# Causal attentions of a decoder: the order of weights, row maxima, roots, values and context turns

## The chip, the cores and the metric

The kernel runs on one core of a Trainium2 chip. The metric is the device time of one execution in microseconds (us). The kernel before was run three times; a further execution was profiled. TensorE multiplies matrices (PE in the profile, PEld for its weight loads), VectorE (DVE), ScalarE (ACT) and GpSimd (POOL) do elementwise work and reductions, and SyncE's queue (SP) issues most DMAs.

## The reference

Eight sequences of 256 tokens with 512 features pass through two decoder layers with post-norm: x = layernorm(x + f(x)) six times. Three of the six functions are causal attentions, and the change is in these:

```python
# 0: differential attention, 16 heads of two 16-wide queries each, 4 key heads
scores = jnp.einsum('bhqd,bhkd->bhqk', q, k) * scale
scores = jnp.where(causal, scores, jnp.finfo(scores.dtype).min)
probs = jax.nn.softmax(scores, axis=-1)
attn_out = jnp.einsum('bhqk,bhkd->bhqd', probs, v)
attn = attn_out[:, 0::2] - lambda_full * attn_out[:, 1::2]
attn = attn * jax.lax.rsqrt(jnp.mean(attn * attn, axis=-1, keepdims=True) + EPS) * ln_w
...
# 3: self attention, 16 heads of 32
a = jax.nn.softmax(scores, axis=-1)
ctx = jnp.einsum('bhqk,bhkd->bhqd', a, v)
...
# 5: attention with keys and values chosen per token by a gate (top 1 of 16)
att = jnp.einsum('bhqd,bkd->bhqk', q, k_shared) * (1.0 / math.sqrt(hd))
y = jnp.einsum('bhqk,bkd->bhqd', jax.nn.softmax(masked, axis=-1), v_shared)
```

Between them stand a long convolution with gating by a context (1), a mixture of eight experts (2) and an attention over context and tokens (4). Everything is in float32.

## The kernel before, in words

The 2048 tokens are 16 tiles of 128. A group (g) is four tiles, so two sequences; there are four groups. All three causal attentions go through one function, `causal_attention` (L1094), each with its own `prepare` (projections of a group) and `finish` (output projection of a sequence, residual, norm). The attentions are called "first" (differential), "second" (self) and "third" (routed) below.

The unit of work is four heads of one sequence. The first attention has 8 units a sequence (`upb`), the others 4; so there are 64, 32 and 32 units. The order of work inside is written out by hand (`manual_schedule`): a loop over slots u, one slot for each unit and some more at the end, says what each engine gets next. Each engine takes its instructions in the order in which the loop issues them.

A unit passes through three steps in different slots:

- `maxima(u)` (L1140): 12 small products give the scores of 4 heads in the PSUM tile ps_q (L1148). ScalarE copies them to `rows` (L1157), GpSimd masks the diagonal blocks (L1159), and VectorE takes negated row maxima (`largest`, L1168) into `neg`. `rows` has two buffers in the first attention and one in the other two.
- After the last unit of a sequence, `split` (L1172) has VectorE write the maxima as three bfloat16 terms, and `turn` (L1185) has TensorE turn them (ps_n, L1190) and ScalarE copy them to `negT` (L1198).
- `weights(u)` (L1200): TensorE makes the transposed scores and adds the turned maxima (ps_k, L1211 and L1220), ScalarE takes the exponential to `pT` (L1228), and GpSimd masks it (L1229) and adds two blocks (L1239). ps_q and ps_k share one PSUM buffer of four banks.
- `products(u)` (L1241): TensorE multiplies with the values (L1254) and with ones for the sums (L1264), into ps_pv, which has one buffer; VectorE takes the reciprocal (L1272) and multiplies (L1278, or L367 and L370 in the first attention).

In slot u the kernel before issues maxima of unit u, then a first part of filling work, the turn (if a sequence has just ended), `sums(u)` (the products of unit u - upb - 1), the row maximum of unit u, the split, what is registered for "mid", the weights of unit u - upb, and the rest of the filling work, then what is registered for "end".

Filling work is TensorE work between the steps. It comes as lists of steps: projections of the next group (`feature_block` and `token_block`, four products of 128x512 each, L182), turns of token tiles (L194, copied by ScalarE, L195), and output projections (ps_o). `fill(budget)` issues steps until a budget per slot is spent, which spreads a group's work over its slots; `need(slot)` issues at once all that is due. Filling projections share three PSUM buffers (the pool `pools`, tag "mm") with turned tiles and ps_n. `begin(g)` asks `prepare` for a group's pieces, half a group ahead.

In the first attention `values` (L323) is due in slot 9 of its group; `turn_context` (L355) in the last group turns the 16 tiles of the context and stores them for a later stage, due in slots 0 to 15. Each tile is loaded by SP into one of two buffers (cx), turned, copied and stored by SP.

`norm_later` (L148) takes moments on VectorE and then the root on GpSimd (`rsqrt`, L140 and L141), and returns the last operation (L154) for later. `add_norm_later` (L208) adds the residual (L211) first. So the two GpSimd operations stand in GpSimd's queue wherever the output projection ended. In the second attention the tokens themselves arrive from the expert stage: `combine` (L1065) gives `load`, `add` (L1081) and a norm.

## Time and profile before

| | us |
|---|---|
| median of 3 runs | 2251.23 |
| lowest and highest | 2244.91 and 2252.63 |
| the profiled execution | 2256.86 |
| its span, first to last instruction | 2255.2 |
| its mean granted TensorE clock | 0.957 of full speed |
| first attention, about | 0 to 500 |
| second attention, about | 1175 to 1545 |
| third attention, about | 1885 to 2255 |

A line of a group in the profile names the source line, the engine, the operation, and the tiles written and read; then follow the number of instructions, their busy time and mean duration, and the idle time of the engine just before them with what ended it. A line of waits has the waiting instruction, what released it, the total in us, the number of waits and the longest. A line of the timeline has start and duration in us, and in brackets the engine's idle time before it. A product in float32 is counted as two instructions there. "PE busy" is modelled for the end of each product.

The groups that are particular to the attentions:

| group | instructions | mean us |
|---|---|---|
| L1157, copy of scores (ACT) | 128 | 1.44 |
| L1228, exponential (ACT) | 128 | 1.45 |
| L1159, mask of rows (POOL) | 128 | 1.10 |
| L1229, mask of pT (POOL) | 128 | 1.09 |
| L1239, sum of two blocks (POOL) | 112 | 1.28 |
| L1168, row maximum (DVE) | 128 | 1.75 |
| L1272, reciprocal (DVE) | 128 | 1.75 |
| L140, first operation of the root (POOL) | 80 | 0.22 |

### The profile page before, as it was taken

To read this page: it belongs to the slowest core of one execution; us is meant where nothing else is said; L and a number is where in the kernel's file an instruction comes from. 1 tells how busy PE (TensorE), PEld (TensorE's weight loads), DVE (VectorE), ACT (ScalarE), POOL (GpSimd) and SP (SyncE) were. 2 spreads that over 40 slices of the span, in tenths; PEclk is the share of its full clock that TensorE was granted. 3 is DMA by queue.
4 is the path that set the end of the run, shared out by engine and by line. 5 is a ranking of instruction groups with operands and counts; after the bars stand their busy time and mean duration, and the time that the engine had idled before them with its cause. 6 is when DMAs were issued, how large, how long until landed. Compare 5 with 4: busy or idle time off the path is not lost. (4 is left out here: it accounts for less than half of the span.)

```text
span 2255.2 us, 35573 instructions
## 1 busy us (share of the span) xinstructions
PE 2072.2 (92%) x14904; PEld 1204.6 (53%) x14904; DVE 1272.1 (56%) x1923; ACT 600.0 (27%) x723; POOL 820.2 (36%) x918
## 2 busy tenths in 40 slices
PE   7889888788999999999959999998999999999996
PEld 4454555444444456555524444446877875545553
DVE  4677666557888964122224656456343343566787
ACT  4555455420000013111114333330110111333332
POOL 2576666555555823000024445333000000232343
PEclk8999999798999999999979999989999999998898
DMA  6899702205214135131131102002000100000000
GB/s 226 339 383 381 260 27 84 73 1 169 83 59 147 57 112 178 61 137 64 47 133 36 58 28 66 1 1 94 29 28 19 38 1 1 1 10 10 10 20 29
DMA packets 110032, 197.56 MB, mean 88 GB/s; under 512 B 7088, under 2 KB 30768, under 8 KB 109872
## 3 DMA queue, kind: packets, MB, share of 16 engines
q1 hardware_dynamic: 104752, 178.49, 23.0%
q0 software_dynamic: 5120, 16.78, 2.2%
q8 instruction: 120, 1.97, 0.4%
q14 instruction: 40, 0.33, 0.0%
HBM read 93.54 MB, written 112.20 MB: 91 GB/s over the span
## 5 line engine op out<-in xcount | busy, mean ns | idle before, releaser
L1272 DVE RECIPROCAL rsum<-ps_pv 128x256 f32<-128x256 f32 x128 | 224.4, 1753 | 290.5 <-PE ps_pv L1264 290.4
L171 PE MATMUL ps_y<-kv,wt 128*128 128x512 f32 x640 | 282.4, 599 | 4.6 <-POOL kv L516 3.8
L1228 ACT ACTIVATE pT<-ps_k 128x1536 f32<-128x1536 f32 x128 | 185.6, 1450 | 303.1 <-PE ps_k L1220 303.1
L1168 DVE TENSOR_REDUCE neg<-rows 128x12 f32<-128x1536 f32 x128 | 223.5, 1746 | 64.9 <-POOL rows L1159 64.9
L1157 ACT COPY rows<-ps_q 128x1536 f32<-128x1536 f32 x128 | 184.1, 1438 | 182.8 <-PE ps_q L1148 153.6
L1229 POOL TENSOR_SCALAR_AFFINE_SELECT pT<-pT 128x1024 f32<-128x1024 f32 x128 | 139.6, 1091 | 240.1 <-ACT pT L1228 239.9
L1159 POOL TENSOR_SCALAR_AFFINE_SELECT rows<-rows 128x1024 f32<-128x1024 f32 x128 | 140.1, 1095 | 221.7 <-ACT rows L1157 221.0
L171 PEld LDWEIGHTS ps_y<-kv,wt 128*128 128x128 f32 x640 | 120.7, 192 | 154.7 <-issue 135.0
L1239 POOL TENSOR_TENSOR pT<-pT 128x512 f32<-128x512 f32 x112 | 143.0, 1277 | 9.3
L1074 POOL DMA_INDIRECT w_l1x<-ys,slots x32 | 31.5, 985 | 267.1 <-DMA ys<-y_m 259.2
L140 POOL TENSOR_SCALAR rstd<-bn_mv 128x1 f32<-128x1 f32 x80 | 17.3, 217 | 299.7 <-DVE bn_mv L146 293.0
L182 PE MATMUL ps_f<-xT,w_l1a 128*128 128x512 f32 x256 | 121.6, 619 | 3.9 <-ACT xT L195 3.9
L182 PE MATMUL ps_t<-w_l1f,xT 128*128 128x512 f32 x256 | 119.8, 606 | 0.1
L989 PE MATMUL po_m<-dn,hT 128*128 (+1 forms) x216 | 101.9, 609 | 1.6
L1264 PE MATMUL ps_pv<-pT,ones_v 128*32 128x256 f32 (+1 forms) x1152 | 88.9, 393 | 10.1 <-POOL pT L1239 9.9
L554 DVE TENSOR_REDUCE yc<-z 128x64 f32<-128x512 f32 x128 | 86.1, 674 | 6.2 <-POOL w_l1a L555 5.8
L182 PEld LDWEIGHTS ps_f<-xT,w_l1a 128*128 128x128 f32 x256 | 47.7, 195 | 58.6 <-issue 51.7
L182 PE MATMUL ps_o<-w_l,yT_b 128*128 128x512 f32 x128 | 69.8, 660 | 9.9 <-DVE yT_b L467 9.3
L1148 PEld LDWEIGHTS ps_q<-kz,qT 32*128 32x128 f32 x1536 | 50.8, 193 | 51.4 <-ACT pT L1228 35.7
L1148 PE MATMUL ps_q<-kz,qT 32*128 32x128 f32 x1536 | 63.3, 296 | 15.4 <-ACT pT L1228 11.8
L1211 PE MATMUL ps_k<-qT,kT 32*128 32x256 f32 (+1 forms) x1024 | 73.6, 374 | 3.9 <-ACT pT L1228 3.4
L1148 PEld LDWEIGHTS ps_q<-kT,qT 32*128 32x128 f32 x1536 | 49.8, 190 | 48.9 <-issue 28.7
(326 smaller groups left out, 3712.4 us busy)
## 6 DMA issues: line engine op xcount, KB each, us to landing
xs<-zero SPq DMA_DIRECT2D x8, 4352.0 KB, 31.4
ys<-zero SPq DMA_DIRECT2D x8, 4352.0 KB, 31.4
filters<-in_L_xattn_k SPq DMA_DIRECT2D x4, 2560.0 KB
first_h<-xs SPq DMA_DIRECT2D x36, 256.0 KB, 2.7
ys<-y_m SPq DMA_DIRECT2D x36, 256.0 KB, 2.0
gu<-in_L_ffn_gate_up_proj SPq DMA_DIRECT2D x3, 2816.0 KB, 20.1
wt<-filters SPq DMA_DIRECT2D x32, 256.0 KB, 2.9
x<-in_x SPq DMA_DIRECT2D x16, 256.0 KB, 4.4
```

The source lines that it names most:

```text
L171: nc.tensor.matmul(ps, lhsT=lhsT(k), rhs=rhs(k), start=(k == 0), stop=(k == n - 1))
L182: nc.tensor.matmul(ps[0], lhsT=lhsT(k), rhs=rhs(k), start=(k == 0), stop=(k == KB - 1))
L989: nc.tensor.matmul(po, lhsT=hT[:m, i, :], rhs=dn[i][:m, bass.ds(e, 1), :], start=(i == 0), stop=(i == len(FCH) - 1),)
L1148: nc.tensor.matmul(block[:, s, j, :], lhsT=q(rows, c, b * S + i * P, P), rhs=k(rows, c, b * S + keys * P, P), start=True, stop=True,)
L1157: nc.scalar.copy(d.rearrange("p j s k -> p s j k"), block)
L1159: nc.gpsimd.affine_select(out=rows, in_=rows, compare_op=ALU.is_ge, fill=-FAR, base=0, pattern=[[0, 8], [-1, P]], channel_multiplier=1,)
L1168: return lambda: nc.vector.tensor_reduce(neg[u // upb % 2][:, :, :, c], d, AX.X, ALU.max, negate=True)
L1228: nc.scalar.activation(p[:, 0:3].rearrange("p j s q -> p s j q"), block, AF.Exp)
L1229: nc.gpsimd.affine_select(out=p[:, 0:2].rearrange("p j s q -> p (j s) q"), in_=p[:, 0:2].rearrange("p j s q -> p (j s) q"), compare_op=ALU ...
L1239: nc.gpsimd.tensor_tensor(p[:, 3], p[:, 1], p[:, 2], ALU.add)
L1264: nc.tensor.matmul(ps[32 * s : 32 * s + 32, 1, j * P :], lhsT=ones_v, rhs=p[:, 1, s, :] if j else first[:, :, s, :], start=(j == 0), stop= ...
L1272: nc.vector.reciprocal(r, ps[:, 1, :])
```

## The change

- The weights of a unit come upb + 1 slots behind its maxima (before: upb), and its products a slot behind that (upb + 2). Each attention has one slot more at its end.
- Inside a slot the order becomes: maxima, first filling work, sums, "mid", weights, begin of a group, turn, rest of the filling work, row maximum, split, "end".
- In the slots after the last unit the weights come ahead of the turn and the sums.
- `norm_later` takes an argument that puts the root elsewhere: in the attentions it is registered for "end" of the slot.
- In the first attention, from the second group on, `values` is the first piece after the turned tiles, and v has three buffers; the 16 context turns are due six slots later.
- In the third attention one more query block is issued ahead of the turn of the keys.

```diff
-    def norm_later(dst, src):
+    def norm_later(dst, src, later=lambda f: f()):
...
-        rsqrt(rstd, mv[:, 1:2], 1.0)
+        later(lambda: rsqrt(rstd, mv[:, 1:2], 1.0))
...
-    def add_norm_later(work, t, ps):
+    def add_norm_later(work, t, ps, at):
...
-        return norm_later(x[t], r)
+        at(1, "mid", norm_later(x[t], r, lambda f: at(0, "end", f)))
...
-            v = work.tile([P, TPG, P], F32, tag="v", name="v")
+            v = work.tile([P, TPG, P], F32, tag="v", name="v", bufs=3)
...
+            values_steps = [(MM, lambda ti=ti: values(ti)) for ti in range(TPG)]
+            if g:
+
+                need.append((0, values_steps))
...
-            need.append((9, [(MM, lambda ti=ti: values(ti)) for ti in range(TPG)]))
+            if g == 0:
+                need.append((9, values_steps))
...
-                    need.append((t, [(TR, lambda t=t: turn_context(work, pools, t))]))
+                    need.append((6 + t, [(TR, lambda t=t: turn_context(work, pools, t))]))
...
-            lag = upb + 1
+            wait = upb + 1
+            lag = wait + 1
...
-                if u >= units:
-
+                if u < units:
+                    largest = maxima(u)
+                    short = min(0.3 * rate, 0.8)
+                    if rate > 2.7:
+                        short += (rate - 2.7) / 2
+                    left = fill(left + short)
+                    sums(u)
+                    happen("mid")
+                    if u >= wait:
+                        weights(u - wait)
+                    if u % upg == upb and u // upg + 1 < NG:
+                        per_group = begin(u // upg + 1)
+                    if u and u % upb == 0:
+                        turn(u // upb - 1)
+                    left = fill(left + rate - short - MM)
+
+                    need(u + 1)
+                    left = fill(left + MM)
+                    largest()
+                    if u % upb == upb - 1:
+                        split(u // upb)
+                else:
+
+                    if u < units + wait:
+                        weights(u - wait)
                     if u == units:
-                        sums(u)
                         turn(B - 1)
-                    if u < units + upb:
-                        weights(u - upb)
-                    if u > units:
-                        sums(u)
+                    sums(u)
                     happen("mid")
                     left = fill(left + rate)
-                    happen("end")
-                    continue
-                largest = maxima(u)
-                if u % upg == upb and u // upg + 1 < NG:
-                    per_group = begin(u // upg + 1)
-                short = min(0.3 * rate, 0.8)
-                if rate > 2.7:
-                    short += (rate - 2.7) / 2
-                left = fill(left + short)
-                if u and u % upb == 0:
-                    turn(u // upb - 1)
-                sums(u)
-                largest()
-                if u % upb == upb - 1:
-                    split(u // upb)
-                happen("mid")
-                if u >= upb:
-                    weights(u - upb)
-                left = fill(left + rate - short - MM)
-
-                need(u + 1)
-                left = fill(left + MM)
                 happen("end")
...
-                    at(first - here + 1, "mid", add)
+                    at(first - here + 1, "mid", lambda add=add: add(lambda f: at(0, "end", f)))
...
-            need.append((0, feature_block(pools, qT, xT, wqkv, 0, 1, HD1**-0.5)))
+            for c in range(1, 3):
+                need.append((0, feature_block(pools, qT, xT, wqkv, 0, c, HD1**-0.5)))
             need.append((0, [(TR, keys_turned)]))
-            for c in range(2, KB):
+            for c in range(3, KB):
                 need.append((c, feature_block(pools, qT, xT, wqkv, 0, c, HD1**-0.5)))
```

## The prediction

> **What bounds the kernel now.** I read the page first, for the engine that is busy throughout; then the table of windows by stage, which gives TensorE's idle time and clock in each; then the waits of TensorE stage by stage; then the timeline of single slots; and last the order of the instructions on each engine in the two kernels.
>
> ```profile
> span 2255.2 us, 35573 instructions
> PE 2072.2 (92%) x14904; PEld 1204.6 (53%) x14904; DVE 1272.1 (56%) x1923; ACT 600.0 (27%) x723; POOL 820.2 (36%) x918
> ```
> ```profile
> core 0: us, PE busy (x) PEld busy (x) DVE busy (x) ACT busy (x) POOL busy (x), PEclk, DMA share, GB/s
> 0.00:500.00 500.00, 425.33 (x5463) 250.17 (x5464) 314.76 (x353) 237.62 (x226) 297.25 (x299) 0.95 0.56 200
> ...
> 1175.00:1545.00 370.00, 346.81 (x2949) 168.93 (x2947) 204.33 (x264) 129.30 (x132) 150.42 (x170) 0.97 0.10 29
> ...
> 1885.00:2255.00 370.00, 333.92 (x3056) 182.82 (x3056) 243.48 (x342) 115.49 (x112) 118.25 (x126) 0.92 0.03 13
> ```
>
> The three causal attentions fill 0 to 500, 1175 to 1545 and 1885 to 2255 us. TensorE is idle in them for 75, 23 and 36 us, and it runs at 0.95, 0.97 and 0.92 of its clock. Only these 134 us, and what slow clock follows them, can be won: the change adds and removes no instruction (the counts of every kind on every engine are equal in the two orders). TensorE's waits in the first stage, one line of the second and two of the third:
>
> ```profile
> PE ps_n L1190 <- DVE terms L1179: 12.0, 6, 2.7
> PE ps_q L1148 <- ACT pT L1228: 11.8, 14, 1.6
> PE ps_o L182 <- DVE yT_b L467: 9.3, 4, 4.3
> ```
> ```profile
> PE ps_pv L1254 <- POOL pT L1229: 9.5, 6, 2.7
> ```
> ```profile
> PE pt_k L1681 <- DVE k L1676: 4.6, 2, 2.3
> PE pt L194 <- DVE sel L1665: 2.7, 1, 2.7
> ```
>
> One slot that turns a batch's maxima, from the timeline:
>
> ```profile
> 205.52 0.95 PE L1148 MATMUL ps_q<-kz,qT 32*128 32x128 f32 x24
> ...
> 206.63 1.18 DVE L1175 TENSOR_TENSOR neg<-neg 128x32 f32<-128x32 f32 x1
> ...
> 209.74 0.20 DVE L1179 CAST terms<-less 128x64 bf16<-128x64 f32 x1
> ...
> 209.99 0.40 PE L1190 MATMUL ps_n<-ident_b,terms 128*32 128x128 bf16 x8 [2.46 <-DVE terms L1179]
> ...
> 210.18 1.50 PE L1254 MATMUL ps_pv<-pT,v 128*32 128x256 f32 x16
> ...
> 213.89 1.45 ACT L1228 ACTIVATE pT<-ps_k 128x1536 f32<-128x1536 f32 x1 [3.07 <-PE ps_k L1220]
> ```
>
> (The cast shown is the last of three; the lines left out on VectorE are the others and the subtractions.) VectorE splits the maxima from 206.6 to 209.9; TensorE stands 2.46 us, then does the 16 products of L1254 in 1.50 us, where the slot before took 0.86 us at 200.70. This slot lasts 10.08 us, from 205.52 to the next L1148 at 215.60. Its neighbours last 6.3 to 7.0.
>
> An ordinary slot is a ring through the one score buffer: 12 maxima products 0.95, copy L1157 1.44, 16 weights products about 1.25, exp L1228 1.45, and small gaps. The shortest slots, such as 228.91 to 234.36, last 5.45 us. From the order I added up each slot as 0.9 + the larger of 1.65 and the products between maxima and weights + 1.25 + the larger of 1.65 and the products behind the weights, with 0.88 us for a filling step of 128x512 and 1.5 us for a slot's L1254 and L1264. All slots but the last of each attention (and the very first) give 366, 312 and 271 us for the kernel before. The timeline has 414 (25.71 to 440.07), 326 (1177.71 to 1503.90) and 297 (1916.01 to 2212.95). So 48, 14 and 26 us are stalls and slow clock.
>
> **What the Trainium skill says.** "TensorE: Matmul & The Clock Gate", Part 1, says that idle time costs twice: after a window of about 3.4 us with little work TensorE falls to half its clock. The 1.50 us against 0.86 us after the stall agrees. "PSUM — Partial Sum Buffer", Engine vs sequencer instructions, says that the queues of ScalarE, VectorE and GpSimd are strictly first in, first out, so an instruction that waits holds up all behind it. The root at 1283.07 below, ahead of a mask whose input was ready, agrees. "SBUF — State Buffer", Who interferes with whom, says that VectorE and GpSimd lock one shared pair of ports. It fits a split operation that takes 1.18 us beside GpSimd's work (206.63) where a like one takes 0.22 us alone, and is why I leave the split's 3.3 us as they are.
>
> **The change part by part.**
>
> *Turn behind the weights.* In the first attention six turns waited for "terms", about 2.5 us in four of the ordinary ones (slots 16, 24, 32, 56: 2.69, 1.54, 2.46, 2.46 = 9.2 us). Behind each, L1254, L1264 and L1211 took 1.50, 1.07 and 0.91 us where 0.86, 0.61 and 0.71 are usual: 1.3 us, times four is 5.2. Gross 14.4 us. In the changed order the turn follows products and weights, some 4 us into the slot, beside the exp. The split then starts behind the maximum at a slot's end: reciprocal from 2.9 us into the slot, 1.76 + 0.45 + 1.75 + 3.3 ends 10.2 us after the slot began, 3.9 us into the next. So it fits barely. I take 4 us back for late turns (bounds 0 and 9). The turn at slot 8 has no products ahead of it in either order and keeps its 2.7 us. Net 10.
>
> *Maximum at the slot's end.* VectorE's adds (L211), which free the filling products' buffers, and the scaling by the roots (L467) now come before the 1.75 us maximum and the split of their slot. The stalls on them were 3.2 us (ps_f at slot 47) and 4.3 us (slot 40). I take 7 of these in the first attention, 2 of 3.0 in the second (bounds 0 and all).
>
> *Values first.* Their first product needs only the first turned tile, where the keys' product waited 1.6 us for the last copy, twice (slots 25 and 42). Gain 3 (0 to 3.2). The third buffer of 2 KB costs no time.
>
> *Context in the last slots.* Stalls for cx were 5.2 us of waits. The new order has three runs of three or four turns in slots 53, 58 and 59 through the same two buffers; two in a row are covered and a third waits for its load. Loads and stores go through SP's queue as before. I take a gain of 1 (bounds -3 and +5).
>
> *One slot further behind.* The sum over slots is unchanged in the first attention (366 and 366): one full slot becomes a maxima-only one, and unevenness eats the rest (one slot has 7.0 us behind its weights, two have none). But one round of weights, exp, mask and products moves into the tail, where nothing fills it. Rounds there last 3.5 to 5.3 us (456.57, 460.51, 463.97, 469.24): 4.5 us lost, and 1.5 us for the turn at the stage's end, which again meets the split. First attention: 10 + 7 + 3 + 1 - 6 = 15 us gained.
>
> *Roots at the end.* GpSimd waited for bn_mv 293 us in all. At 1283.07 it does so ahead of the mask of pT whose exp had ended long before, and the products stand behind it. They lost 9.5 and 2.7 us to pT in the second attention; I take 5. The root's wait at a slot's end holds only the next slot's mask of rows, which needs a copy 2.5 us into that slot. The second attention gains 2 more at its first turn (1.6 us of wait in the slot from 1208.63). Its slot sum falls from 312 to 307, but 4.1 us of that are ps_o steps that go to the tail: gain 1. The extra round costs 3.5. Rows have one buffer here, so a copy waits for the maximum of the slot before; a slot has 5.1 us before its weights, 3.5 before the copy must start, so I take 1. Second attention: 5 + 2 + 2 + 1 - 3.5 - 1 = about 6 gained.
>
> *Third attention.* pt_k waited 2.3 us twice and the clock fell; another query block (4 x 0.88 us) now lies ahead of it: gain 5. The slots that turn tokens and compute gates (from 1940.92, 2024.57, 2113.65) take 15.3, 21.4 and 16.7 us against 9.6, 11.1 and 8.5 by the sum; the turns come behind the weights now, where exp and not the split holds their buffers. I take 7 of 24 (bounds -5 and 15). Costs: the query block ahead of the first maxima 3.5, less 0.7 from the slot sum; two slots with nothing to fill them (the fourth of a group) where the weights would be ready 2.6 us in but the copy waits for the late maximum, 2.5 each, 5; the extra round at the kernel's very end 4, its turn 1. Net 12 - 12.8, about 1 lost.
>
> Sum: 15 + 6 - 1 = 20 us. The profiled execution took 2256.86 us, so 2237 in its terms. It lies 5.6 us above the median 2251.23 of the three runs; on the median I forecast 2231 us.
>
> **Rivals.**
>
> *The turn waits where it now stands (no change).* The split ends no earlier, and the same VectorE queue decides: 3.9 us against 4 us leaves no reserve. Against it: exp runs meanwhile. If the 10 us come back and the tails cost 5 us more, 5 us remain: about 2246.
>
> *The late maximum blocks the single rows buffer (slower).* It bears on the 62 slots counted in the second and third attention. It decides once the maximum ends later than 3.5 us into the next slot, or 1 us in an unfilled one. For it: VectorE is busy 243 of 370 us in the third stage, and the page of waits has ACT's copy held by neg already, 8.4 us in the second stage and 7.7 in the third. Against: the mean slot leaves room. At 0.65 us a slot it costs 40 us: 2231 + 40 = 2271.
>
> *The clock recovers too (better).* The clock missed 0.05 x 500 and 0.08 x 370, together 55 us, in the first and third stage. If a third more comes back than I booked, 18 us: 2213.
>
> **How the numbers follow.** Forecast 0.48, no change 0.15, slower 0.25, better 0.12. The forecast's own range is 2214 to 2247, mostly from the bounds above. The range 2208 to 2272 takes in the slower case and most of the better one. A measurement of this kernel tells about 0.3%, 7 us. Faster: 0.44 of the forecast, 0.12 and 0.03, 0.59. Same: 0.04 and 0.10, 0.14. Slower: 0.25 and 0.02, 0.27.
>
> **What would show it.** ps_n's wait for terms should fall from 12 us to about 6 in the first stage; ps_pv's wait for POOL's pT should halve in the second; pt_k's should vanish. If ACT's copy waits for neg more than 25 us in the last two stages together, the slower rival holds. If ps_n still waits 12 us, the first does. The forecast is wrong if the first stage ends less than 8 us earlier.

## The result and the profile after

Over 20 runs of each kernel the changed one takes 2246.65 us (median; 2238.15 to 2256.63), the one before 2256.09 us (2244.91 to 2268.8). The ratio is 0.9953, with a 95% interval of 0.9937 to 0.9969: 10.6 us are gained, where 20 were forecast. The sign was right, and the size about double what came.

The profiled run of the changed kernel took 2239.09 us, 7.6 less than its own median, while the profiled run before (2256.86) lies at its median. So the two profiles differ by 17.8 us, more than the kernels do. The sizes below are therefore taken from ratios where there are any, and from single stretches of several profiles otherwise.

The page of the changed kernel (engines' busy time, and one group with its mean in ns and the idle time ahead of it):

```profile
span 2237.4 us, 35572 instructions
PE 2057.1 (92%) x14904; PEld 1203.5 (54%) x14904; DVE 1272.0 (57%) x1923; ACT 598.9 (27%) x723; POOL 823.8 (37%) x918
...
L1161 ACT COPY rows<-ps_q 128x1536 f32<-128x1536 f32 x128 | 184.1, 1438 | 237.6 <-DVE neg L1172 130.0
```

TensorE has 15 us less of busy time for the same 14904 instructions, and the work of the other engines is the same to 4 us. The third line shows what has grown: of the 237.6 us that ScalarE is idle ahead of its 128 copies of scores, 130.0 end when the row maximum of the unit before is done (17.7 in the kernel before). (Lines have moved by a few: copy L1157 is now L1161, maximum L1168 is L1172, terms L1179 is L1183, products L1254 are L1258.)

The table of windows for the three attentions, which now lie at 0 to 500, 1165 to 1530 and 1865 to 2237 us:

```profile
0.00:500.00 500.00, 431.98 (x5478) 254.88 (x5479) 313.36 (x355) 238.00 (x227) 299.01 (x300) 0.94 0.56 200
...
1165.00:1530.00 365.00, 343.95 (x2976) 172.23 (x2975) 217.96 (x274) 130.00 (x135) 160.80 (x176) 0.99 0.12 38
...
1865.00:2237.00 372.00, 325.70 (x3022) 177.44 (x3022) 239.35 (x336) 113.32 (x108) 117.52 (x124) 0.93 0.03 12
```

The second attention is tighter: its clock went from 0.97 to 0.99, and TensorE's idle time from 23 to 21 us in a window 5 us shorter. The third stands still for 46 us, where it stood for 36.

For a finer account I cut each profile at the first and the last maxima product (L1152; L1148 before) of each attention. "To the second" and "to the third" hold the tail of one attention, the stages after it, and the start of the next.

| us | first | to the second | second | to the third | third | to the end |
|---|---|---|---|---|---|---|
| before | 419.7 | 737.6 | 326.2 | 412.1 | 296.9 | 42.2 |
| changed | 405.8 | 737.9 | 307.6 | 420.8 | 297.5 | 45.3 |
| changed, another chip (changed_again) | 408.7 | 752.0 | 307.7 | 422.5 | 302.4 | 46.6 |

The first attention gained 13.9 us and the second 18.6. The way to the third lost 8.7, the end 3.1, and the third itself gained nothing. The two profiles of the changed kernel also show the scatter: 6.2 us in the third attention with its end.

A stretch from first to last maxima isn't the whole of an attention: at the longer distance one unit's weights and products leave it for the tail (54 of TensorE's instructions, 4746 instead of 4800 in the first attention). So it pays to add the tail, up to the first product of the stage that follows (ps_y for the first attention, ps from xT for the second):

| us | first with tail | second with tail | third with end |
|---|---|---|---|
| before | 504.6 | 372.5 | 339.1 |
| changed | 493.7 | 359.1 | 342.8 |
| changed_again | 496.8 | 359.2 | 349.1 |

So the first attention gained 8 to 11 us and the second 13, and the third lost 4 to 10 us. Besides, the way from the first gate product (ps_g) to the first maxima of the third, with the query block now ahead, grew from 27.3 to 32.3 and 34.0 us.

TensorE's waits in the first stage (waited for, us in total, times, longest):

```profile
PE ps_q L1152 <- ACT pT L1232: 14.6, 15, 1.6
PE ps_n L1194 <- DVE terms L1183: 11.6, 5, 5.7
PE pt L195 <- DMA cx<-in_ctx: 7.1, 4, 2.3
```

The 9.3 us for yT_b are gone. The wait for terms, forecast to halve, is 11.6 us where it was 12.0, but in other places: the four ordinary turns named in the forecast went from 9.2 to about 2.1 us, slot 8 rose from 2.7 to 3.74, and one turn of 5.7 us is in the tail. A turn in the new order, from the timeline:

```profile
149.50 0.95 PE L1152 MATMUL ps_q<-kz,qT 32*128 32x128 f32 x24 [1.02 <-ACT pT L1232]
...
151.43 0.86 PE L1258 MATMUL ps_pv<-pT,v 128*32 128x256 f32 x16
...
153.31 0.71 PE L1215 MATMUL ps_k<-qT,kz 32*128 32x256 f32 x8
...
153.74 1.02 DVE L1183 CAST terms<-less 128x64 bf16<-128x64 f32 x1
...
154.54 1.45 ACT L1232 ACTIVATE pT<-ps_k 128x1536 f32<-128x1536 f32 x1 [2.58 <-PE ps_k L1224]
...
154.81 0.29 PE L1194 MATMUL ps_n<-ident_b,terms 128*32 128x128 bf16 x8 [0.40 <-DVE terms L1183]
```

The split still runs to 154.8, 5.3 us into the slot, but products and weights go ahead of it, and TensorE waits 0.40 us where it waited 1.54 in the same slot (24) before. The slot takes 7.45 us (to 156.95) instead of 7.80. The slot quoted before with 10.08 us is slot 32. It hardly pays:

```profile
203.73 0.95 PE L1152 MATMUL ps_q<-kz,qT 32*128 32x128 f32 x24
...
209.46 0.30 PE L1194 MATMUL ps_n<-ident_b,terms 128*32 128x128 bf16 x8 [1.32 <-DVE terms L1183]
...
210.18 4.46 PE L183 MATMUL ps_f<-xT,w_l 128*128 128x512 f32 x10
```

Its wait fell from 2.46 to 1.32 us and its products take 0.86 instead of 1.50 us, but it holds five products of filling work at its end now, and it lasts 10.84 us (to 214.56).

The second stage, one line of TensorE's waits:

```profile
PE ps_pv L1258 <- POOL pT L1233: 1.9, 1, 1.9
```

It was 9.5. The third stage, TensorE's largest wait, which was 0.5 us at one slot before:

```profile
PE ps_k L1215 <- ACT rows L1161: 13.8, 11, 3.1
```

The weights wait for the copy of the scores. What the copy waits for is in ScalarE's waits, third window:

```profile
ACT rows L1161 <- DVE neg L1172: 82.8, 19, 6.5
```

The second window has 47.2 us at 11 slots. In the whole kernel before it was:

```profile
ACT rows L1157 <- DVE neg L1168: 17.7, 8, 5.9
```

The forecast set 25 us as the mark of the slower rival; 130 came. One such slot, from the timeline (start, duration, engine, line; in brackets what ended the wait):

```profile
1994.12 0.95 PE L1152 MATMUL ps_q<-kT,qT 32*128 32x128 f32 x24
...
1994.41 0.66 DVE L1667 TENSOR_TENSOR sel<-ps_t,itop 128x512 f32<-128x512 f32 x1
...
1996.06 1.74 DVE L1172 TENSOR_REDUCE neg<-rows 128x12 f32<-128x1536 f32 x1
...
1997.89 1.44 ACT L1161 COPY rows<-ps_q 128x1536 f32<-128x1536 f32 x1 [6.23 <-DVE neg L1172]
...
1999.38 0.71 PE L1215 MATMUL ps_k<-qT,kT 32*128 32x256 f32 x8 [3.09 <-ACT rows L1161]
...
2002.07 1.67 PE L1152 MATMUL ps_q<-kT,qT 32*128 32x128 f32 x24 [1.54 <-ACT pT L1232]
...
2003.67 1.51 PE L1258 MATMUL ps_pv<-pT,v_r 128*32 128x256 f32 x16
```

This is slot 11, one of the two that have no filling work. Its maxima are in the score buffer at 1995.1. The copy that would empty it writes into the one rows buffer, which VectorE has yet to read for the slot before: that maximum starts at 1996.06, behind a reciprocal, adds, moments and the reading of filling products, which keep VectorE at work without a pause from 1987.51 on. The copy starts at 1997.89, the weights wait 3.09 us for the score buffer, and then come slow products: the next slot's maxima take 1.67 instead of 0.95 us, its L1258 1.51 instead of 0.86. The slot lasts 7.95 us, and 5.2 with the old order (third_old, below).

The two slots without filling work, 11 and 19, make up 6.2 of the 13.8 us. Of the rest, 4.2 us lie in slots 9, 14 and 21, which have filling work:

```profile
1979.95 0.71 PE L1215 MATMUL ps_k<-qT,kT 32*128 32x256 f32 x8 [1.03 <-ACT rows L1161]
...
2031.61 0.71 PE L1215 MATMUL ps_k<-qT,kT 32*128 32x256 f32 x8 [1.36 <-ACT rows L1161]
...
2109.07 0.84 PE L1215 MATMUL ps_k<-qT,kT 32*128 32x256 f32 x8 [1.84 <-ACT rows L1161]
```

### The profile page after: what moved, and what is told of

It reads as the page before. It is cut to its first block, busy times and chain, and to the rows that moved or that the text cites. A ratio compares the mean times of both kernels' runs of the same rounds, so it can differ in the third digit from the quotient of the medians.

```text
span 2237.4 us, 35572 instructions
## 1 busy us (share of the span) xinstructions
PE 2057.1 (92%) x14904; PEld 1203.5 (54%) x14904; DVE 1272.0 (57%) x1923; ACT 598.9 (27%) x723; POOL 823.8 (37%) x918
## 5 line engine op out<-in xcount | busy, mean ns | idle before, releaser
L1172 DVE TENSOR_REDUCE neg<-rows 128x12 f32<-128x1536 f32 x128 | 223.0, 1742 | 56.2 <-POOL rows L1163 56.2
L1161 ACT COPY rows<-ps_q 128x1536 f32<-128x1536 f32 x128 | 184.1, 1438 | 237.6 <-DVE neg L1172 130.0
L1152 PE MATMUL ps_q<-kz,qT 32*128 32x128 f32 x1536 | 64.8, 301 | 18.1 <-ACT pT L1232 14.6
L1152 PEld LDWEIGHTS ps_q<-kT,qT 32*128 32x128 f32 x1536 | 51.5, 196 | 54.1 <-issue 27.2
L1152 PEld LDWEIGHTS ps_q<-kz,qT 32*128 32x128 f32 x1536 | 52.0, 198 | 51.4 <-ACT pT L1232 34.3
L1215 PEld LDWEIGHTS ps_k<-qT,kT 32*128 32x128 f32 x1024 | 42.6, 195 | 56.4 <-ACT rows L1161 30.3
## 6 DMA issues: line engine op xcount, KB each, us to landing
gu<-in_L_ffn_gate_up_proj SPq DMA_DIRECT2D x3, 2816.0 KB, 19.8
```

Source lines behind the costliest of these rows:

```text
L1152: nc.tensor.matmul(block[:, s, j, :], lhsT=q(rows, c, b * S + i * P, P), rhs=k(rows, c, b * S + keys * P, P), start=True, stop=True,)
L1161: nc.scalar.copy(d.rearrange("p j s k -> p s j k"), block)
L1172: return lambda: nc.vector.tensor_reduce(neg[u // upb % 2][:, :, :, c], d, AX.X, ALU.max, negate=True)
L1215: nc.tensor.matmul(block[:, s, at, :], lhsT=k(rows, c, b * S + j * P, P), rhs=q(rows, c, b * S + j * P, P * (2 - j)), start=True, stop=False,)
```

## The experiments

All are edits of the changed kernel and compute the whole reference. Each ratio is to the kernel before on the same chip; the runs are spread over four chips.

| run | ratio | 95% interval |
|---|---|---|
| changed_again | 0.9961 | 0.9950 to 0.9972 |
| first_old | 1.0014 | 0.9999 to 1.0030 |
| second_old | 0.9960 | 0.9948 to 0.9972 |
| third_old | 0.9893 | 0.9871 to 0.9914 |
| third_before | 0.9884 | 0.9861 to 0.9908 |
| rows_two | 0.9923 | 0.9899 to 0.9947 |
| max_mid_third | 0.9942 | 0.9922 to 0.9962 |
| roots_at_once | 0.9944 | 0.9920 to 0.9967 |
| first_near | 0.9884 | 0.9848 to 0.9921 |
| first_max_mid | 0.9927 | 0.9899 to 0.9954 |
| values_context_back | 0.9852 | 0.9817 to 0.9887 |
| third_old_rows_two | 0.9870 | 0.9841 to 0.9899 |
| values_back | 0.9860 | 0.9840 to 0.9880 |
| context_back | 0.9905 | 0.9889 to 0.9921 |
| best | 0.9848 | 0.9831 to 0.9865 |

### The order, one attention at a time

One attention at a time was given the old distance and the old order of a slot; 0.001 of the ratio is 2.26 us. Three kernels, with 'a', 's' or 'r' in the first line (first, second, third attention):

```diff
-            wait = upb + 1
+            old = name in ('r',)
+            wait = upb if old else upb + 1
...
+                if old:
+                    largest = maxima(u)
+                    if u % upg == upb and u // upg + 1 < NG:
+                        per_group = begin(u // upg + 1)
...
+                    if u and u % upb == 0:
+                        turn(u // upb - 1)
+                    sums(u)
+                    largest()
+                    if u % upb == upb - 1:
+                        split(u // upb)
+                    happen("mid")
+                    if u >= wait:
+                        weights(u - wait)
```

> The changed kernel with the old slot order and distance in the first attention only (values first and late context turns stay). Theory: the order is worth 8 to 10 of the 14 us that the profiles show in its first 63 slots: ratio about 0.999, and ps_n waits for terms at five turns for 2.5 us each again. Rival: values first and the context gave most: ratio about 0.997.

> The changed kernel with the old slot order and distance in the second attention only. If the 18.6 us that one profile shows between its first and last maxima come from the order, and 5 go in its tail: ratio about 1.001. If roots at the end give them (they stay here): ratio about 0.996 and the stretch stays near 308 us. If the one profile exaggerates: the stretch is between.

> The changed kernel with the slot order and the distance of the kernel before in the third attention only (roots at the end and the second query block ahead of the keys stay). Theory A (the new order loses time in the third attention, some 7 us from its first to its last maxima and in its tail): ratio to before about 0.992. Theory B (the third attention is even, as forecast within 1 us): ratio 0.995, and its stretch from the first maxima to the end stays about 343 us.

> The changed kernel once more, as the base for the runs beside it. If the earlier ratio of 0.9953 holds on this chip: 0.994 to 0.9965, and the third attention takes 343 to 350 us from its first maxima to the end.

The last is the changed kernel itself, as the measure for the runs beside it. Against its 0.9961, the old order in the first attention is 0.0053 or 12 us slower, more than either forecast; in the second it is no different, and in the third 0.0068 or 15 us faster, more than the 7 us of theory A. So by ratio the new order is worth 12 us in the first attention, nothing in the second, and costs 15 us in the third, each give or take 4 or 5 us.

The profiles agree on the third: with its end it takes 329.7 to 334.5 us in the six runs that have third_old's code there, and 342.8 to 349.1 in five that have the changed one. In the second attention with its tail, thirteen runs with the changed code and one rows buffer take 359.1 or 359.2 us and second_old 356.7: the new order costs 2.4 us there. In the first with its tail, first_old takes 498.8 us and eight runs with the changed code 492.2 to 497.7, 494.6 in the mean: 4 us instead of the ratio's 12. Another 4 us of its loss against changed_again lie in the stages between the first attention's tail and the second, where the edit changes nothing. So the order gains in the first attention, but how much stays open.

### The third attention

*rows_two*: two buffers for the scores' copy in all three attentions, with one less of another tile to make room.

```diff
-        r = work.tile([P, D], F32, tag="row", name="res", bufs=3)
+        r = work.tile([P, D], F32, tag="row", name="res", bufs=2)
...
-                d = work.tile([P, 3, 4, P], F32, tag="rows", name="rows", bufs=2 if gather else 1)
+                d = work.tile([P, 3, 4, P], F32, tag="rows", name="rows", bufs=2)
```

> The changed kernel with two rows buffers in the second and third attention too; to make room the residual tile (res) has two buffers instead of three. Theory A (the single rows buffer under the late maximum ate the missing gain): ScalarE's copy waits for neg fall from 130 us to under 30 us, TensorE's waits of ps_k for rows in the third attention from 13.8 us to under 2, and the ratio to the kernel before falls from 0.9953 to about 0.990 (10 to 12 us). Theory B (the copies' waits lie mostly beside filling work, and the gain went in the longer tails and in front of the third attention): the waits fall the same way and the ratio stays within 0.9935 to 0.996.

*max_mid_third*: one buffer as in the changed kernel, but in the third attention the maximum is back behind the sums; distance and turn stay.

```diff
                     sums(u)
+                    if name == "r":
+                        largest()
+                        if u % upb == upb - 1:
+                            split(u // upb)
                     happen("mid")
...
-                    largest()
-                    if u % upb == upb - 1:
-                        split(u // upb)
+                    if name != "r":
+                        largest()
+                        if u % upb == upb - 1:
+                            split(u // upb)
```

> The changed kernel with the row maximum and the split right behind the sums again, in the third attention only; one rows buffer, turn behind the weights and the longer distance stay. Theory A (the late maximum holds the single rows buffer): the third attention's stretch to the end falls by 10 us or more, as with two buffers (336 us), and the waits of ACT's copies for neg fall from 83 us to under 25. Rival (distance and turn cost the time): it falls by less than 4 us.

*third_before*: third_old, and the query block behind the turn of the keys again.

```diff
-            for c in range(1, 3):
-                need.append((0, feature_block(pools, qT, xT, wqkv, 0, c, HD1**-0.5)))
+            need.append((0, feature_block(pools, qT, xT, wqkv, 0, 1, HD1**-0.5)))
             need.append((0, [(TR, keys_turned)]))
-            for c in range(3, KB):
+            for c in range(2, KB):
```

> The changed kernel with the third attention wholly as before: slot order and distance, and one query block ahead of the turn of the keys; the roots stay at the end. If the query block ahead costs what was forecast (3.5 us, and its gain at pt_k is small with the old order): 2 to 4 us less than with the slot order alone undone, ratio about 0.988. If the block ahead pays by itself (it ends pt_k's waits of 2.3 us): 2 to 5 us more, about 0.991.

TensorE's wait for the copy in the third attention is 13.5 us at 10 slots in changed_again. In rows_two:

```profile
PE ps_k L1215 <- ACT rows L1161: 0.7, 2, 0.3
```

In max_mid_third, where the maximum is earlier but the buffer single:

```profile
PE ps_k L1215 <- ACT rows L1161: 4.1, 4, 1.6
```

and ScalarE's waits there:

```profile
ACT rows L1161 <- DVE neg L1172: 19.2, 7, 4.1
```

The third attention with its end takes 335.8 us in rows_two and 339.1 in max_mid_third. Five profiles with the changed third attention (the root apart in one) have 342.8, 344.2, 349.0, 349.0 and 349.1. Either edit alone takes most of the wait away, so it needs both: a single buffer and a late maximum. Its price is 0.0038 or 9 us by rows_two's ratio, between what theories A and B expected. 2.7 of these lie in the second attention, which has two buffers as well in that run and takes 356.4 us with its tail instead of 359.1; the 47.2 us that ScalarE waits there cost no more than that. By the profiles the third attention loses 7 to 13 us. rows_two also has one res buffer less, which was not tried alone. max_mid_third's ratio alone, 4 us better with overlapping intervals, would not settle it.

The timelines, cut at each slot's first maxima product, show which slots pay (us; slots counted from 0 in the third attention, those not listed lie within some 2 us of each other; third_old is the old order, with the query block ahead):

| slot | third_before | third_old | rows_two | changed_again |
|---|---|---|---|---|
| 3 and 4 (turns tokens) | 20.7 | 23.0 | 19.8 | 19.3 |
| 7 (last of a group) | 14.2 | 15.1 | 16.8 | 16.8 |
| 11 (nothing to fill) | 7.0 | 5.2 | 5.2 | 7.9 |
| 12 (turns tokens) | 21.4 | 15.3 | 14.9 | 13.6 |
| 15 (last of a group) | 14.2 | 15.1 | 17.7 | 17.7 |
| 19 (nothing to fill) | 7.5 | 5.2 | 5.2 | 8.8 |
| 20 (turns tokens) | 16.7 | 13.9 | 11.6 | 12.3 |
| 21 | 8.5 | 6.5 | 7.0 | 12.1 |
| 23 (last of a group) | 18.6 | 22.0 | 22.8 | 22.9 |

The single buffer takes 2.7 and 3.6 us in the two unfilled slots and 5.1 in slot 21, of which 1.85 are a wait of its own and the rest slow products; what is left is spread. From third_old to rows_two, both on one chip, the token slots fall by 5.9 us, the last slots of the groups rise by 5.1, and the whole is the same: 287.2 and 287.4 us. This is filling work that has moved. Slots 4, 12 and 20 hold 3, 3 and 1 products of 128x512 fewer in the new order, and slots 7, 15 and 23 hold 2, 3 and 1 more, at 0.86 us each. TensorE's waits in slots 4, 12 and 20 don't fall: 9.9 us in third_old, 11.0 in rows_two. So beside the query block the new order wins nothing in the slots that turn tokens.

The fair comparison has two rows buffers on both sides: the third attention with its end takes 335.8 us in rows_two, and 326.4 and 327.4 in the two runs with the old order and two buffers (third_old_rows_two and best, below). The new order costs 9 us here even without the wait, most of it at the end, where the extra round and its turn stand. From the last maxima to the end it is 45.3 to 48.5 us in seven runs with the new order and 40.4 to 44.9 in ten with the old one, 4 us apart in the mean. On the way to the third, rows_two is 4.3 us longer than third_old; runs with the same code there differ by 3 us, so nothing follows from it.

The query block costs 3.4 us ahead of the first maxima by one pair of profiles (417.4 in third_before, 420.8 in third_old; 420.7 to 423.7 in the other runs of that code) and gives 3 to 8 us back in the rest (337.4, and 329.7 to 334.5). By ratio the two are the same.

### The second attention

*roots_at_once*: the root is issued behind its moments again; the order stays.

```diff
-        later(lambda: rsqrt(rstd, mv[:, 1:2], 1.0))
+        rsqrt(rstd, mv[:, 1:2], 1.0)
```

> The changed kernel with the roots issued where the moments are taken, as before, and all else as changed. Theory C (the roots at a slot's end give most of the second attention's gain, 14 of 18 us from first to last maxima, since the stretch stayed 312 us with the old slot order there): that stretch rises from 308 to about 320 us and the ratio from 0.9953 to about 1.000. Rival (as forecast, 5 us, since the split and the weights' distance do the rest): the stretch stays below 314 us and the ratio below 0.998.

GpSimd's waits for the moments between 1165 and 1500 us, in the kernel before, then in second_old (old order, roots at the end), then in roots_at_once (new order, roots at once), then in the changed kernel:

```profile
POOL rstd L140 <- DVE bn_mv L146: 73.3, 19, 8.7
```
```profile
POOL rstd L140 <- DVE bn_mv L146: 31.0, 17, 6.0
```
```profile
POOL rstd L140 <- DVE bn_mv L146: 46.4, 18, 5.9
```
```profile
POOL rstd L140 <- DVE bn_mv L146: 7.1, 5, 2.3
```

Both still leave GpSimd much of its wait. What counts is whether TensorE waits for it. From first to last maxima of the second attention:

| us | before | second_old | roots_at_once | changed |
|---|---|---|---|---|
| the stretch | 326.2 | 311.9 | 308.1 | 307.6 |
| TensorE's waits (over 0.15 us) | 16.7 | 7.5 | 8.2 | 8.6 |
| of these, for GpSimd's pT | 7.6 | none | 0.8 | none |
| TensorE busy | 310.0 | 305.1 | 300.3 | 299.7 |
| its instructions | 2582 | 2582 | 2528 | 2528 |
| with the tail | 372.5 | 356.7 | 359.6 | 359.1 |

Roots at the end without the new order give 14.3 us: 9.2 of waits, and 4.9 because the same 2582 instructions take less time. The new order without the late roots takes the waits for pT away as well. (Some 4 to 5 us of its 18.1 are the round that went to the tail.) So either alone takes GpSimd's stall off the path, and the second adds nothing. With the tail the late roots are worth 15.8 us, and the new order on top of them costs 2.4. Theory C, that most of the gain goes when the roots are at once again, fell with this. The rival's marks held, though not its 5 us. Over the whole kernel the late roots add nothing to the new order: 0.9944 without them, 0.9961 with them, overlapping.

### The first attention

Here the base is third_old (0.9893; first attention 404.7 us), so that the third's losses don't cover anything. *first_near*: old distance in the first attention and the turn ahead of the weights, with the maximum still at the slot's end. *first_max_mid*: the reverse, only the maximum and split back behind the sums.

```diff
-            wait = upb if old else upb + 1
+            wait = upb if old or gather else upb + 1
...
                     happen("mid")
+                    if gather and u and u % upb == 0:
+                        turn(u // upb - 1)
                     if u >= wait:
                         weights(u - wait)
```

```diff
                     sums(u)
+                    if gather:
+                        largest()
+                        if u % upb == upb - 1:
+                            split(u // upb)
                     happen("mid")
```

> The same with the third as before, values and context as changed, but in the first attention the weights at the old distance and the turn ahead of them (products a slot behind the weights, maximum still at the slot's end). Forecast (the turn behind the weights gives 10 us there): the stretch rises from 404 to at least 412 us and ps_n waits for terms about 3 us at each of the ordinary turns. Rival (the maximum's place gives it): below 408 us.

> The same with the third as before, and in the first attention the row maximum and split right behind the sums, with the turn behind the weights and the longer distance kept. Forecast (the maximum's place gives 7 us there through adds and scalings that no longer wait): the stretch rises from 404 to about 410 us and waits for res and yT_b come back. Rival (the turn gives all): the stretch stays within 2 us of 404, or falls, since the terms are ready earlier.

The first attention takes 415.1 us in first_near and 413.9 in first_max_mid, somewhat more than either forecast. But first_near has one round more inside the stretch, so the two are compared with their tails: 497.3 and 501.4 us, beside 492.2 to 497.7 in the eight runs with the changed code, 494.6 in the mean. Distance and turn together are worth some 3 us, and by ratio nothing (0.9884 beside third_old's 0.9893). The late maximum is worth 6.8 us, and 8 by ratio, the intervals overlapping a little. In first_max_mid TensorE's wait for yT_b is back:

```profile
PE ps_o L183 <- DVE yT_b L471: 9.5, 4, 3.8
```

The late maximum is not the only way to lose it: first_old, with the maximum in the middle and everything else of the order old too, has 3.6 us of it.

*values_context_back* puts both edits of the filling back, *values_back* and *context_back* one each, on third_old.

```diff
-            if g:
-
-                need.append((0, values_steps))
...
-            if g == 0:
-                need.append((9, values_steps))
+            need.append((9, values_steps))
...
-                    need.append((6 + t, [(TR, lambda t=t: turn_context(work, pools, t))]))
+                    need.append((t, [(TR, lambda t=t: turn_context(work, pools, t))]))
```

> The changed kernel with the third attention's slot order and distance as before, and in the first attention values due in slot 9 and context turns due from slot 0 as before. Forecast (values 3 us, context 1 us): the first attention's stretch from first to last maxima rises from 404 to 406 to 410 us, waits of keys for the last xT copy (1.6 us) come back, ratio 0.990 to 0.992. Rival (values and context give most of the first attention's gain): above 412 us, ratio 0.994.

> Third attention in the old slot order, values due in slot 9 again, context turns late as changed. With both undone the first attention's stretch fell from 404.7 to 397.7 us. If values first costs it (it forces queries into bursts: 11.3 us in slot 47, and leaves slots 37 to 39 unfilled): the stretch falls to about 399 us. If the context does: it stays at 403 to 406 us.

> Third attention in the old slot order, context turns due from slot 0 again, values first as changed. If the late context costs it (three runs of turns through two buffers, slots 53, 58 and 59): the stretch falls to about 400 us and the slots 53 to 60 together by 5 us. If values first does: it stays at 403 to 406 us.

The first attention takes 397.7, 398.5 and 400.4 us, where third_old takes 404.7 and other runs of its code there 403.5 to 409.7. That both edits undone would shorten it was in neither branch of the first expectation. With the values first, slots 32 to 48 take 121.7 us; in values_back 112.9. By ratio values_back is 0.0033 or 7 us faster than third_old, with intervals that overlap a little. With the context as before on both sides, values_context_back is 0.0053 or 12 us faster than context_back, with intervals that just miss each other. So the values first, booked as a gain of 3, cost some 6 us or more. The waits for the turned tiles' last copy did go, as forecast: one of 1.52 us is back in values_back at slot 43. What replaced them is in the timeline of the changed kernel. Four steps moved ahead of the keys and queries push those toward the group's end, so that slot 47 has to take what is left while others have nothing. Slot 47:

```profile
306.94 0.95 PE L1152 MATMUL ps_q<-kz,qT 32*128 32x128 f32 x24
...
311.13 2.84 PE L183 MATMUL ps_o<-w_l,yT_b 128*128 128x512 f32 x6
...
313.81 4.46 PE L183 MATMUL ps_f<-xT,w_l 128*128 128x512 f32 x10
...
318.19 0.95 PE L1152 MATMUL ps_q<-kz,qT 32*128 32x128 f32 x24
```

That slot takes 11.25 us, and 5.9 in values_back, whose slot 48 takes 3.0 more in turn. Slot 37 (from 242.38) has nothing to fill it; what follows, in slot 38:

```profile
247.62 0.95 PE L1152 MATMUL ps_q<-kz,qT 32*128 32x128 f32 x24 [1.63 <-ACT pT L1232]
...
250.27 1.51 PE L1258 MATMUL ps_pv<-pT,v 128*32 128x256 f32 x16 [1.11 <-POOL pT L1233]
```

TensorE waits twice, and its products then take 1.51 us. The context stays open: undone, the stretch is 4.3 us shorter, and slots 53 to 60 fall from 64.4 to 55.8, as expected if it costs. But the ratio (0.9905 against 0.9893, overlapping) is no better, and with the values back too the stretch is only 0.8 us shorter. On the same chip the stages between the first attention's tail and the second take 654.8 and 655.0 us in the two runs with the context undone, and 650.4 with it late: what it costs in the attention may come back there. This was not tried.

### A better version

*third_old_rows_two* is third_old with two rows buffers in the third attention; *best* is that with values and context back.

```diff
-                d = work.tile([P, 3, 4, P], F32, tag="rows", name="rows", bufs=2 if gather else 1)
+                d = work.tile([P, 3, 4, P], F32, tag="rows", name="rows", bufs=1 if name == "s" else 2)
```

> The third attention's slot order and distance as before, with two rows buffers in it; all else as changed. If rows matter with the maximum in the middle too (ACT waited 7.7 us for neg there): 2 to 4 us less than with one buffer, ratio 0.988. If the single buffer only hurts under the late maximum: ratio within 0.001 of 0.9893, stretch of the third to the end 330 us.

> Third attention in the old slot order with two rows buffers, values and context as before, the rest as changed. If the savings seen apart add up: the stretch of the first 398 us, the third to the end 327 us, ratio 0.984 to 0.986. If one is only a draw of the clock: above 0.988.

The second buffer under the old order takes the third attention with its end from 329.7 us (334.5 at most in runs of that code) to 326.4. In the last kernel the first attention's stretch is 399.8 us and the third with its end 327.4, and the ratio is where it was expected if the savings add up. It takes 2220.47 us beside 2256.99 for the one before, 34 us less by its ratio of 0.9848 (0.9831 to 0.9865), and its interval lies wholly below that of the changed kernel. Its page:

```profile
span 2223.8 us, 35592 instructions
PE 2057.8 (93%) x14904; PEld 1197.5 (54%) x14904; DVE 1275.0 (57%) x1923; ACT 598.2 (27%) x723; POOL 823.1 (37%) x918
```

TensorE's busy time is that of the changed kernel, and the 13.6 us between the spans are idle time saved.

## Why the prediction was right in sign and double in size

The step that failed is the third attention. It was booked at -1 us, and it lost some 16: a gain of 7 us in the slots that turn tokens did not come, and the single rows buffer cost about twice what was booked. The second attention gave 7 us more than booked. Errors in opposite directions partly cancelled, so that half the forecast came out is in part luck.

**First attention, forecast +15, measured 8 to 11** (with its tail):

- Turn behind the weights, 10, less the tail, 6: 4 were booked for the two, and undoing them costs 3 us by the profiles and nothing by ratio. The gross gain was misread. The 5.2 us for slow products behind four turns held at one turn only, slot 32, where L1254 took 1.50 us. At the other three it took 0.82, after waits of 2.69, 1.54 and 2.46 us; two of them:

```profile
101.58 0.30 PE L1190 MATMUL ps_n<-ident_b,terms 128*32 128x128 bf16 x8 [2.69 <-DVE terms L1179]
101.70 0.82 PE L1254 MATMUL ps_pv<-pT,v 128*32 128x256 f32 x16
...
381.98 0.29 PE L1190 MATMUL ps_n<-ident_b,terms 128*32 128x128 bf16 x8 [2.46 <-DVE terms L1179]
382.10 0.82 PE L1254 MATMUL ps_pv<-pT,v 128*32 128x256 f32 x16
```

- By its own mark the first rival would hold, since ps_n's wait for terms stayed at 11.6 us. The mark was badly chosen: four turns lost 7 of their 9.2 us of waits, but slot 8 and the turn in the tail, booked at 2.7 and 1.5 us, stand 3.74 and 5.7. In the tail that wait lies where the extra round is; the tail grew by 3.1 us (84.8 to 87.9 from the last maxima to ps_y).
- Maximum at the slot's end, 7: 6.8. The yT_b wait went with it and came back without it.
- Values first, +3: -6 or worse. The step counted only the wait that goes, and not that the same steps are then missing in later slots and bunch in others.
- Context, 1: nothing by ratio.
- These parts don't add up to the whole. first_old, which has none of the order's gains and pays for the values first, is still 5.8 us better than the kernel before (498.8 and 504.6). It has the late roots. The prediction booked them at nothing in the first attention, and what they give there without the new order was not tried.

The forecast was to be wrong if the first stage ended less than 8 us earlier; its last maxima come 11.7 us earlier (440.07 and 428.35).

**Second attention, forecast +6, measured 13** (with its tail). The late roots were booked at 5 and gave 15.8; the order's terms were booked at about nothing together and cost 2.4. The step took 5 of the 12.2 us of waits for pT. Those inside the stretch, 7.6 us, all went, and so did another 1.6 for terms. It also left out that the products get faster with the waits gone, 4.9 us, which the step on the turns did count. The slot named for it, 1283.07, is not one that shows the loss: TensorE had filling work there until 1285.36, and the products began at 1285.41. ps_pv's wait for POOL's pT fell from 9.5 to 1.9 us in the whole stage, more than the half forecast.

**Third attention, forecast -1, measured about -16.** Old order and old block together give 0.9884 where the change gives 0.9961, 17 us. The terms:

- Slots that turn tokens, booked at +7: nothing. These slots did get 6 to 7 us shorter, but only because seven filling products left them, and the last slots of the groups got 5 us longer with six of these. TensorE's waits in them did not fall (9.9 us in third_old, which has the query block and the old order; 11.0 in rows_two and 8.0 in changed_again).
- Single rows buffer, booked at 5 us as two unfilled slots of 2.5: about 9 by rows_two's ratio, 2.7 of them in the second attention, and 7 to 13 in the third by the profiles. The two slots came as 2.7 and 3.6, but TensorE waited at 11 slots, 13.8 us in all. The rule that only unfilled slots are hit left out VectorE's queue: where it is full, the maximum comes late in filled slots too, and TensorE waits in the next one (1.0 to 1.8 us in slots 9, 14 and 21). The slower rival named just this mechanism, and its mark, 25 us, was passed with 130; I put it at 40 us over both attentions, four times what it cost.
- Tail, booked at 5: about 4, from the last maxima to the end.
- Query block ahead, booked at +5 for pt_k's waits and -2.8: the waits vanished and the block cost 3.4 us or more ahead; by ratio it gives nothing.

Buffer and tail make about 13 of the 16 us; the rest is within the scatter. The first attention's 8 to 11, the second's 13 and the third's -16 make 5 to 8 us, and 10.6 were measured. Of the rivals, "the turn waits where it now stands" (2246) has the right time for the wrong reason: the turns did move out of the way, and the loss was in the third attention. The range, 2208 to 2272, held the time.

Open: how much the order is worth in the first attention (4 us by profiles, 12 by ratio), what the late roots give there, and the context's share.

## What to carry to other kernels

An operation that frees a single buffer sets when the next slot's copy can start; before it is moved behind other work of its engine, count every slot whose queue ahead of it is long, not only those with an empty engine. The same edit can gain in one loop and lose in the next that has one buffer less: try each loop alone (here 12, 0 and -15 us by ratio). When work is moved earlier to remove a wait of 1.6 us, ask which later slot it used to fill. When a slot gets shorter, count its products before calling it a gain: they may have gone to another slot, or out of the stretch that you measure.

## What the runs showed of the hardware

After some waits the small products took about 1.75 times as long, 1.51 us for 16 that take 0.86, in both attentions alike. In the changed kernel this followed waits of 3.09 and 1.54 us within 5 us in the third attention, and of 1.63 and 1.11 us in the first. The length of the last wait alone doesn't decide it: in the kernel before, 2.46 us were followed by 1.50 us at one turn and by 0.82 at another, and 2.69 by 0.82. What else does was not tried. All these waits are shorter than the window of about 3.4 us that the prediction quotes. So the price of slow products behind a wait has to be read at each place.

The way from the first to the second attention, in which the change edits little but the first's tail, took 737 to 744 us in the runs beside which the kernel before had a median of 2256.99 and in the first profile of either kernel, and 748 to 757 us on three other chips, where the kernel before had 2268.9 to 2269.8. In one of those, changed_again, TensorE has this wait between 850 and 950 us

```profile
PE po_m L993 <- ACT hT L986: 10.3, 1, 10.3
```

and ScalarE, whose output it is, this one:

```profile
ACT hT L986 <- remote: 10.9, 1, 10.9
```

No engine of the core is named as the releaser. All twelve profiles from the three chips have such a line, of 8.9 to 10.9 us; the other five, the first profile of either kernel among them, have none. The pause is about the difference between the chips' medians (12 us), and its cause was not tried; a ratio to a run on the same chip leaves it out, and a comparison of two profiles from different chips does not.
